# Two attention layers on one core: eighth score ahead of the fourth mixing, input piece issued a half earlier

## The chip, the cores and the metric

The program runs on one core of a Trainium2 chip, in one launch. The metric is the device time of that launch in microseconds, the median of several executions. The engines named are TensorE (PE, its weight loads PEld), VectorE (DVE), ScalarE (ACT), GpSimd (POOL) and SyncE (SP), which issues nearly all DMA transfers.

## The reference, cut to what matters

Eight images of 512 channels and 32 x 32 positions (T = 1024) pass through two attention layers with 8 heads of 64 channels. Each layer is given a group normalization of its input, and its result is added to the input. All is float32. The first layer is ordinary softmax attention with its own second normalization. The second one, in which the change lies, mixes the heads' scores before the softmax and normalizes the softmax's result over each image and head:

```
q, k, v = w_q @ y, w_k @ y, w_v @ y                     # y: normalized input, split in 8 heads
attn = einsum('bhdq,bhdT->bhqT', q, k) * scale          # scores
attn = einsum('gh,bhqT->bgqT', w_head, attn)            # mixing of the heads
attn = softmax(attn, axis=-1)
attn = (attn - mean(attn)) / sqrt(var(attn) + eps) * in_gamma + in_beta   # per image and head
out  = einsum('bhqT,bhdT->bhqd', attn, v)
x    = x + w_proj @ out + b_proj
```

## The kernel before, in words

**Layer 2's loop.** An outer loop runs over the eight images (instances). For each, an object `Attention1` works in blocks `p` of 128 queries, eight blocks and a last round that only finishes. A block is cut into four quarters `t`; the method `step(p, t, ag)` (line 1847) writes out by hand what is issued in a quarter. The order in that text is the order in which each engine gets its instructions; there is no planner. Three blocks are in flight at once: `step(p, ...)` makes the scores of block `p`, mixes and exponentiates block `p - 1`, and multiplies blocks `p - 1` and `p - 2` by the values. An `Agenda` calls further work (projections of values, normalizations of the next image, projection of its keys) at numbered slots between the quarters.

**Scores.** `scores(p, i)` (line 1621) makes the eighth part `i` of a block's scores: for two heads, against one half `kh` of the 1024 keys. Parts 0 to 3 are the first half, 4 to 7 the second. Each takes a two-bank tile of PSUM from a ring of three tiles (`m_psum`, pool `ps1_m`), and ScalarE copies it into the tile `raw[kh]` in SBUF (line 1640).

**Regrouping.** In the mixing the heads have to lie on partitions. So `regroup(p, kh, s)` (line 1642) issues two DMA transfers of 256 KB from `raw[kh]` into a slot of the tile `re_t`; four values of `s` make up a half. A half can only go out when the copies of its four scores are done, since each transfer reads from all of them. The first half's slots go round five places, the second half's are four fixed ones, so a transfer of the second half waits until the mixing of the block before has read that slot. At the end of quarter 1 the first half's first three slots are issued, at the end of quarter 2 the fourth, at the end of quarter 3 the second half's four. All go through the SP queue, in order.

**Mixing.** `mix(p, s)` (line 1656) multiplies the regrouped scores with the mixing weights. It takes two tiles of the same ring of three, and ScalarE makes the exponentials of each (line 1678) into a tile `e` of a ring of two. VectorE transposes them (`flip`, line 1686) and takes their moments (`moments`, line 1698). In the kernel before, `mix` issues the matmuls and the first tile's exponential, and returns a function that issues the second tile's exponential, so that the caller can put something between the two. The mixing `mix(p - 1, 0)` is issued in quarter 0, after three scores of block `p` and 64 products of the values; it needs slot 0 of both halves, the second of which was issued at the end of the quarter before.

**Pieces.** `piece()` (line 1650) issues one transfer from a list: for each image but the last, the four parts of the next image's input (`y_piece`, line 1333) and two parts of the weights for its keys (`left_piece`, line 1302), 512 KB each; for the last image four parts of the projection's weights (`p_piece`, 256 KB each). One is issued in each block from `p = 1` until the list is empty. The input's tile has one buffer, and the parts are normalized from slot 20 on, that is from quarter 0 of block 5.

The other transfers of a block are a small one and its broadcast of 256 KB on POOL's queue (lines 1772 and 1779).

Of the kernel before, what the change touches and what calls it, by code (L numbers as in the profile page):

```python
# [467 lines left out]
def tile_two_attention_layers(  # L468
# [798 lines left out]
    with ExitStack() as l1:  # L1267
# [15 lines left out]
        def m_psum(nm):  # L1283
            return ps_m.tile([P, 2, FB], F32, tag="m", name=nm)
# [156 lines left out]
        def k_leave():  # L1441
            for fn in due:
                fn()
            due.clear()
# [168 lines left out]
        class Attention1:  # L1613
# [42 lines left out]
            def mix(self, p, s):  # L1656

                b = self.b
                first = (4 * p + s) % NF
                halves = re_t[:, first : NF + s + 1 : NF + s - first]  # L1660
                ps = [m_psum(f"m1_{b}_{p}_{s}_{h}") for h in range(2)]
                for c in range(4):
                    for a in range(4):
                        rows = slice(a * 32, a * 32 + 32)
                        nc.tensor.matmul(  # L1665
                            ps[a // 2][c * 32 : c * 32 + 32, a % 2].rearrange(
                                "p (r h k) -> p h r k", r=2, h=2
                            ),
                            wmix[rows].rearrange("p g i -> p (g i)"),
                            halves[rows].rearrange(  # L1670
                                "p h r (kb c k) -> p c h (r kb) k", c=4, k=32
                            )[:, c],
                            start=True, stop=True, tile_position=(a * 32, c * 32),
                        )
                e = self.e[p, s] = epool.tile([P, 2, 4, 2 * P], F32, tag="e", name=f"e1_{b}_{p}_{s}")

                def exponentials(h):
                    nc.scalar.activation(  # L1678
                        e[:, :, 2 * h : 2 * h + 2].rearrange("p r a k -> p a r k"),
                        ps[h].rearrange("p a (r k) -> p a r k", r=2), AF.Exp,  # L1680
                    )

                exponentials(0)
                return lambda: exponentials(1)

            def flip(self, p, s):

# [159 lines left out]
            def step(self, p, t, ag):  # L1847

                new, old, older = p < NT, p >= 1, p >= 2
                if t == 0:  # L1850
                    if new:
                        for i in range(3):
                            self.scores(p, i)
                    if older:
                        self.values(p - 2, 0, 2, 3)
                        self.leave(p - 2, 0)
                        self.sums(p - 2)
                        if p % 2 == 0 and p >= 4:
                            self.divide(p // 2 - 2, nc.gpsimd)
                    if old:  # L1860
                        self.mix(p - 1, 0)()
                    ag.run(4 * p - 0.5)
                elif t == 1:
                    if older:
                        self.values(p - 2, 1, 0)
                        self.flip(p - 1, 0)
                        self.totals(p - 2)
                        self.moments(p - 1, 0)
                    if new:
                        self.scores(p, 3)  # L1870
                    if old:
                        self.mix(p - 1, 1)()
                    ag.run(4 * p + 0.5)
                elif t == 2:
                    if older:
                        self.values(p - 2, 1, 1)
                    if new:
                        self.scores(p, 4)
                        self.scores(p, 5)
                    if old and not new:  # L1880
                        self.mix(p - 1, 2)()
                    ag.run(4 * p + 1.5)
                    if older:
                        self.values(p - 2, 1, 2, 3)
                        self.leave(p - 2, 1)
                    if old and new:
                        self.mix(p - 1, 2)()
                else:
                    if new:
                        self.scores(p, 6)  # L1890
                        if old:
                            self.values(p - 1, 0, 0)
                            second = self.mix(p - 1, 3)
                        self.scores(p, 7)
                        if old:
                            second()
                            self.values(p - 1, 0, 1)
                    else:
                        self.mix(p - 1, 3)()
                        self.values(p - 1, 0, 0, 1)  # L1900
                    ag.run(4 * p + 2.5)
                k_leave()
                if p == 1 or old and t:
                    self.flip(p - 1, t)
                    self.moments(p - 1, t)
                if new:
                    for kh, s in (
                        (), ((0, 0), (0, 1), (0, 2)), ((0, 3),), ((1, 0), (1, 1), (1, 2), (1, 3)),
                    )[t]:
                        self.regroup(p, kh, s)  # L1910
                if old and t == 2:
                    self.piece()
                ag.run(4 * p + t)

# [155 lines left out]
```

## Time and profile before

| what | value |
|---|---|
| median of 3 runs | 4051.5 us (4041.93 to 4057.18) |
| the profiled execution | 4047.25 us |
| its span, first to last instruction | 4045.5 us |
| granted TensorE clock | 0.994 |
| busy: TensorE, VectorE, ScalarE, GpSimd | 3895.9, 2833.2, 1966.6, 128.5 us |
| layer 2 (from its first regrouping) | from 1806 us on |
| HBM read and written | 197.16 and 46.92 MB |

Rows in the profile give a start in us from the span's beginning, a duration, the engine, the line in the kernel, the operation, what it writes and reads, and how many instructions are merged (x8). A bracket at the end is the idle time of that engine before the row, with what ended it. "SPq" rows are DMA issues. A row of a group on the page has the busy time, the mean duration in ns of one instruction, and after the bar the idle time before such instructions. Matmul rows count the passes that a float32 product takes, so one score of 4 products has 8. Shares are averages over layers with different limits: VectorE's 70% is 21.00 us of the 22.25 us from 2753.75 to 2776.00, a block of layer 2, in which the DMA engines' mean share is 0.93.

### The profile page before, as it was taken

How to read it: one execution, taken by the hardware profiler on the slowest of the kernel's cores; microseconds unless marked ns; L12 is line 12 of the kernel's file. 1: busy time of each engine (PE TensorE's matmuls, PEld its weight loads, DVE VectorE, ACT ScalarE, POOL GpSimd, SP SyncE). 2: the span in 40 equal slices, each digit the busy share in tenths (PEclk: the TensorE clock that was granted, in tenths of full speed). 3: DMA queues.
4: the chain of work that ended last, by engine and by line, in shares of the span. 5: the costliest groups of instructions: out<-in, count | busy, mean ns of one | idle time of the engine just before them, and what ended most of it. 6: DMA issues, size and time to landing. Idle time of an engine off the chain costs nothing. (4 is left out here: it accounts for less than half of the span.)

```text
span 4045.5 us, 95879 instructions
## 1 busy us (share of the span) xinstructions
PE 3895.9 (96%) x41932; PEld 1835.3 (45%) x41932; DVE 2833.2 (70%) x4124; ACT 1966.6 (49%) x2431; POOL 128.5 (3%) x150
## 2 busy tenths in 40 slices
PE   8999999999999999999999999999999999999997
PEld 4353535343444435334544545545544445445354
DVE  4748475756666575747848858759769679588597
ACT  1717263545445362616517537437257166175274
POOL 0000000000000000000000000000001000000010
PEclk9999999999999999999999999999999999999998
DMA  3313131211111211228638638559468287386384
GB/s 126 112 47 116 45 118 48 87 51 54 66 66 58 77 54 61 77 84 208 184 115 213 197 109 221 169 136 226 144 169 221 96 210 202 109 218 189 109 219 125
DMA packets 245884, 519.10 MB, mean 128 GB/s; under 512 B 47313, under 2 KB 54481, under 8 KB 238801
## 3 DMA queue, kind: packets, MB, share of 16 engines
q1 hardware_dynamic: 238912, 497.95, 42.9%
q0 software_dynamic: 6544, 14.94, 1.7%
q8 instruction: 331, 5.42, 0.6%
q14 instruction: 97, 0.79, 0.1%
HBM read 197.16 MB, written 46.92 MB: 60 GB/s over the span
## 5 line engine op out<-in xcount | busy, mean ns | idle before, releaser
L1693 DVE STREAM_TRANSPOSE et<-e 128x2048 f32<-128x2048 f32 x256 | 587.4, 2294 | 137.1 <-ACT e L1678 131.8
L1720 PEld LDWEIGHTS a<-et,v 128*64 128x64 f32 x16384 | 512.0, 139 | 296.7 <-issue 230.8
L1704 DVE BATCH_NORM_STATS2 bn<-e 128x6 f32<-128x512 f32 x1024 | 633.9, 675 | 0.0
L1089 ACT ACTIVATE e<-s 128x1024 f32<-128x1024 f32 x512 | 497.2, 1026 | 234.0 <-PE s L1084 231.9
L1678 ACT ACTIVATE e<-m 128x1024 f32<-128x1024 f32 x512 | 502.9, 1023 | 203.0 <-issue 94.6
L1720 PE MATMUL a<-et,v 128*64 128x64 f32 x16384 | 560.4, 225 | 14.8 <-DVE et L1693 10.4
L1640 ACT COPY raw<-s 128x1024 f32<-128x1024 f32 x480 | 470.1, 1018 | 205.8 <-PE s L1628 172.6
L1097 DVE TENSOR_TENSOR zacc<-zacc,e 128x1024 f32<-128x1024 f32 x384 | 468.8, 1221 | 90.4 <-ACT e L1089 68.1
L1628 PE MATMUL s<-k,q 64*64 64x512 f32 x4096 | 515.8, 608 | 6.3 <-DVE q L1493 3.1
L1084 PE MATMUL s<-q,k 64*64 64x512 f32 x4096 | 490.1, 593 | 2.3 <-ACT e L1089 2.3
L1110 PE MATMUL a<-e,v 64*64 64x512 f32 x4096 | 484.1, 589 | 0.0
L1665 PE MATMUL m<-re,wmix 32*32 32x512 f32 x8192 | 322.7, 605 | 81.4 <-DMA re<-raw 67.8
L1110 PEld LDWEIGHTS a<-e,v 64*64 64x64 f32 x4096 | 156.7, 133 | 282.8 <-issue 282.2
L1084 PEld LDWEIGHTS s<-q,k 64*64 64x64 f32 x4096 | 147.9, 133 | 275.1 <-issue 240.5
L1628 PEld LDWEIGHTS s<-k,q 64*64 64x64 f32 x4096 | 128.1, 132 | 263.7 <-issue 98.7
L1454 PE MATMUL pv<-wv,y 128*128 128x512 f32 x480 | 212.1, 597 | 0.0
L1736 ACT COPY q<-a 64x256 f32<-64x256 f32 x256 | 93.8, 366 | 179.2 <-PE a L1720 177.0
L1665 PEld LDWEIGHTS m<-re,wmix 32*32 32x32 f32 x8192 | 73.5, 103 | 171.6 <-ACT e L1678 53.3
L1772 POOL DMA_DIRECT2D zd<-rz x56 | 34.7, 619 | 3476.0 <-DVE r L1784 3476.0
L1454 PEld LDWEIGHTS pv<-wv,y 128*128 128x128 f32 x480 | 89.3, 190 | 116.9 <-issue 110.3
L1458 ACT COPY v<-pv 128x512 f32<-128x512 f32 x30 | 17.6, 585 | 218.7 <-PE pv L1454 218.7
L1095 DVE TENSOR_TENSOR zacc<-e,e 128x1024 f32<-128x1024 f32 x64 | 78.3, 1223 | 57.2 <-ACT e L1089 57.2
(315 smaller groups left out, 3944.6 us busy)
## 6 DMA issues: line engine op xcount, KB each, us to landing
re<-raw SPq DMA_DIRECT2D x1024, 256.0 KB
left_q<-left_q SPq DMA_DIRECT2D x17, 1792.0 KB
left_p<-left_p SPq DMA_DIRECT2D x17, 1792.0 KB
left_k<-left_k SPq DMA_DIRECT2D x10, 1792.0 KB
x<-in_x_dram SPq DMA_DIRECT2D x32, 512.0 KB
rzb<-zd SPq DMA_DIRECT2D x128, 128.0 KB
x<-x SPq DMA_DIRECT2D x64, 256.0 KB
y<-x SPq DMA_DIRECT2D x32, 512.0 KB
```

The source lines that it names most:

```text
L1084: nc.tensor.matmul(ps[c * D : c * D + D, m], k[r, hp, k0 : k0 + D], q[r, hp, ts(f, FB)], start=True, stop=True,)
L1089: nc.scalar.activation(e[i], ps, AF.Exp, scale=S0 * S0)
L1097: nc.vector.tensor_add(zacc[g], zacc[g], e[i])
L1110: nc.tensor.matmul(acc[g][a][m * D : m * D + D], v[rows, kc, ts(2 * hp + m, D)], e[i][rows, m], start=(kc == 0), stop=(kc == NG - 1),)
L1454: nc.tensor.matmul(ps[:, m], y_t[b][:, c, ts(2 * i + m, P)], w[:, c], start=(c == 0), stop=(c == NCC - 1),)
L1628: nc.tensor.matmul(ps[c * D : c * D + D, m], qo_t[b][r, p, hp, ts(c, D)], k_t[b][r, hp, ts(kh, FB)], start=True, stop=True,)
L1640: nc.scalar.copy(dst, ps)
L1665: nc.tensor.matmul(ps[a // 2][c * 32 : c * 32 + 32, a % 2].rearrange("p (r h k) -> p h r k", r=2, h=2), wmix[rows].rearrange("p g i -> p ( ...
L1678: nc.scalar.activation(e[:, :, 2 * h : 2 * h + 2].rearrange("p r a k -> p a r k"), ps[h].rearrange("p a (r k) -> p a r k", r=2), AF.Exp,)
L1693: nc.vector.transpose(self.et[p, u].rearrange("p kb (r st a) g q -> p st kb r (a g q)", r=2, st=2)[:, st], self.e[p, s].rearrange("p r a ( ...
L1704: nc.vector.bn_stats(self.bn[p][:, s, a], e[:, :, a].rearrange("p r k -> p k r"))
L1720: nc.tensor.matmul(acc[two * D : two * D + D, s].rearrange("p (x q) -> p x q", q=4), v_t[b][:, kb, ts(g, D)], et[:, kb, :, g], start=(kb = ...
```

## The change

Two things move; nothing is added or taken away.

- In quarter 3, the order of issue becomes: score 6, values, score 7, fourth mixing, values. Before it was score 6, values, fourth mixing, score 7, values, with the second exponential of that mixing held back until after score 7. The function that `mix` returned is gone, and both exponentials are issued by `mix` itself everywhere; in the other quarters this is the same order as before. On ScalarE the last quarter's order becomes copy 6, copy 7, exponential, exponential, instead of copy 6, exponential, copy 7, exponential.
- The piece is issued in quarter 0 instead of quarter 2. On the SP queue, it stood between a block's first-half regrouping (8 transfers) and its second-half regrouping (8 transfers). Now it stands ahead of the block's first half, right behind the second half of the block before.

On VectorE and GpSimd the order of the instructions is unchanged.

```diff
                 exponentials(0)
-                return lambda: exponentials(1)
+                exponentials(1)
...
                     if old:
-                        self.mix(p - 1, 0)()
+                        self.mix(p - 1, 0)
...
                 else:
                     if new:
                         self.scores(p, 6)
                         if old:
                             self.values(p - 1, 0, 0)
-                            second = self.mix(p - 1, 3)
                         self.scores(p, 7)
                         if old:
-                            second()
+                            self.mix(p - 1, 3)
                             self.values(p - 1, 0, 1)
                     else:
-                        self.mix(p - 1, 3)()
+                        self.mix(p - 1, 3)
                         self.values(p - 1, 0, 0, 1)
...
-                if old and t == 2:
+                if old and t == 0:
                     self.piece()
```

More of the change, by code (lines that the diff above doesn't have):

```diff
@@ L1871, in step @@
                     if old:
-                        self.mix(p - 1, 1)()
+                        self.mix(p - 1, 1)
                     ag.run(4 * p + 0.5)
@@ L1880, in step @@
                     if old and not new:
-                        self.mix(p - 1, 2)()
+                        self.mix(p - 1, 2)
                     ag.run(4 * p + 1.5)
@@ L1886, in step @@
                     if old and new:
-                        self.mix(p - 1, 2)()
+                        self.mix(p - 1, 2)
                 else:
```

## The prediction

> **What bounds the kernel now.** I read the page first (engine shares, then the costliest groups), then the waits, then the timelines of layer 1, where all of the change lies. Page:
>
> ```profile
> PE 3895.9 (96%) x41932; PEld 1835.3 (45%) x41932; DVE 2833.2 (70%) x4124; ACT 1966.6 (49%) x2431; POOL 128.5 (3%) x150
> ...
> L1665 PE MATMUL m<-re,wmix 32*32 32x512 f32 x8192 | 322.7, 605 | 81.4 <-DMA re<-raw 67.8
> ```
>
> TensorE hardly rests, and the one large idle item in its rows is the mixing's, released by the regrouping DMA. TensorE's timeline of one block (instance 3; the block's last quarter begins at 2768.31 with the seventh score, the next block's first quarter at 2773.75):
>
> ```profile
> 2768.31 1.11 PE L1628 MATMUL s<-k,q 64*64 64x512 f32 x8
> 2769.35 1.15 PE L1720 MATMUL a<-et,v 128*64 128x64 f32 x32
> 2770.43 1.29 PE L1665 MATMUL m<-re,wmix 32*32 32x512 f32 x32
> 2771.64 1.09 PE L1628 MATMUL s<-k,q 64*64 64x512 f32 x8
> 2772.66 1.15 PE L1720 MATMUL a<-et,v 128*64 128x64 f32 x32
> 2773.75 2.81 PE L1628 MATMUL s<-k,q 64*64 64x512 f32 x24
> 2776.48 2.08 PE L1720 MATMUL a<-et,v 128*64 128x64 f32 x64
> 2780.07 1.15 PE L1665 MATMUL m<-re,wmix 32*32 32x512 f32 x32 [1.50 <-DMA re<-raw]
> ```
>
> Everything runs back to back except before the block's first mixing at 2780.07. ScalarE and the SP queue show why:
>
> ```profile
> 2768.58 1.94 ACT L1678 ACTIVATE e<-m 128x1024 f32<-128x1024 f32 x2 [0.48 <-ACT q L1736]
> 2770.41 1.02 ACT L1640 COPY raw<-s 128x1024 f32<-128x1024 f32 x1
> 2771.89 1.02 ACT L1678 ACTIVATE e<-m 128x1024 f32<-128x1024 f32 x1 [0.46 <-PE m L1665]
> 2772.80 1.01 ACT L1640 COPY raw<-s 128x1024 f32<-128x1024 f32 x1
> ```
> ```profile
> 2765.93 5.04 SPq L1646 DMA_DIRECT2D re<-raw  x4
> 2771.02 1.26 SPq L1337 DMA_DIRECT2D y<-x  x1
> 2773.84 18.20 SPq L1646 DMA_DIRECT2D re<-raw  x16
> ```
>
> The eighth score's copy ends at 2773.81 and the second half's regrouping is issued at 2773.84; the 512 KB input piece went in 2.82 us before it. The mixing starts 6.23 us after that issue. I call its idle time the boundary wait, measured as the start-to-start gap less the usual 0.15. Over the 56 boundaries that follow a changed quarter, the timelines give 61.1 us for the first six of each instance (48 waits; median 1.41, longest 2.77) and 23.0 us for the seventh (2.9 each; it has no next scores as cover): 84 us, 2% of the span.
>
> **What the Trainium skill says.** "Perfetto Trace Analysis", section Tensor Engine Instruction: ScalarE and VectorE are strict FIFO. The trace agrees: the eighth copy (2772.80) stands behind an exponential (2771.89), although its score began at 2771.64. "DMA: Bandwidth & Descriptors", section Queues, rings and completion order: each DMA engine takes a ring's descriptors in order, and engines finish a DMA independently. The trace agrees: with a 512 KB piece ahead, issue to mixing took 5.2 to 7.4 us, mostly about 6; at the seventh boundaries, without one, mostly 4.4 to 4.7, and 5.2 to 5.4 in two of eight. "PSUM — Partial Sum Buffer", section Specifications: eight 2 KiB banks; three two-bank score/mixing tiles and two one-bank tiles fill them, so the ring of three stays. No run here shows that count.
>
> **Part 1: eighth score ahead of the fourth mixing.** No instruction is added. On TensorE the order becomes score 7, values, score 8, mixing 4, values. A gap depends on what it follows (0.15 after values, 0.52 after a score or a mixing, start to start), so the sum of the quarter is the same. Score 8 moves to 2770.43; its last product starts 0.50 later and a copy follows a score's last start by 0.65 (2782.44 + 0.50 to 2783.59), so copy 8 is ready at 2771.58. ScalarE is free of copy 7 at 2771.43. Copy 8 then ends at 2772.60 and the regrouping goes out at 2772.63: **1.2 us earlier** (rounded from 1.21).
>
> What is pushed back: mixing 4 starts at 2771.45. The ring of three gives score 8 the first tile of mixing 3 (exponential done by 2769.6), and mixing 4 the second tile of mixing 3 (done by 2770.52) and score 7's (copied by 2771.43). Its second tile is wanted at 2771.50 and released about 0.11 after the copy's end, 2771.54: 0.04 us of stall, against the 0.15 that mixing 4 loses now to the exponential before it (0.70 instead of 0.55 to issue). Free, with 0.1 us of cover; a longer delay costs its length 56 times, since values, the next three scores and the boundary mixing are queued behind it on TensorE. Exponentials 4 run 2772.75 to 2774.80, where they end at 2774.74 now; VectorE's transpose of them starts at 2775.53 after other work. Behind them on ScalarE are the next block's copies, 2775.93. The last regrouping of the half waits for mixing 4 to have read its slot (about 2772.7), but is not issued before about 2776.5.
>
> **Part 2: the piece.** On SP it moves from between the two halves to ahead of the first half, so right behind the previous block's second half. 46 pieces (six of 512 KB in each of seven instances, four of 256 KB in the last) leave the queue in front of the 8 regroupings. In the solid stretch after 2776, about 2 MB moved in 7 us, 0.29 MB a us: 1.8 us a piece. Its new cover: DMA share falls to 0.07 in 2784.0 to 2785.5. Second half 2.1 MB (7.2 us) from 2773.8, piece 1.8, ends by about 2783; the next first half is issued at 2784.6 now and about 2783.1 with the wait gone. If that cover is gone, the first half has until the next boundary, over 10 us. SP's own issue (0.8 us) falls before a wait for a copy. Each transfer also waits on SP for the eighth one before it; for the piece that is the half's first, landed by then. The first piece overwrites a buffer that a value projection (7 us of TensorE, right behind the half's last score) reads last; SP issues the half for some 5 us of that, and behind the piece only the next first half queues, which has no data yet.
>
> **Sum.** Mixing can begin at 2778.57, 5.9 us after the new issue; without a piece ahead it needs about 4.5. So the first six waits go: 61.1. Left over: nine waits above 1.9 us, cut by 1.8 to 1.9 where only the piece sets the landing, 2; one wait of 1.65 in the last instance with no piece ahead, 1. VectorE takes some: between a block's first transposes its work is 20.1, 20.2, 20.8, 21.2, 20.3 us in blocks 1 to 5, TensorE without waits about 20.7 to 21.4. It idles on the exponential of the same mixing:
>
> ```profile
> 2783.38 2.31 DVE L1693 STREAM_TRANSPOSE et<-e 128x2048 f32<-128x2048 f32 x1 [1.71 <-ACT e L1678]
> ```
>
> Where its idle time is the smaller of the two, mostly blocks 3 and 4 with a normalization, the difference is lost: 3. At the seventh boundary VectorE does not idle in the first seven instances (subtractions for the next projection follow), so 2.9 down to 1.7 on TensorE buys nothing there; in the last it idles 1.7, so 1.2 gained. 61.1 - 2 - 1 - 3 + 1.2 = **56 us**. I take off 2 for TensorE's own 1.3 us "issue" pauses, a few of which the waits now absorb (both ends: 0 to 8): 54. The profiled execution took 4047.25 us (span 4045.5): 3993. The median of the runs is 4.25 above: 4051.5 - 54 = **3997.5**.
>
> **Rivals.**
> 1. Half the gain. VectorE's 70% hides that it is within 1 us of TensorE in layer 1; if its lag spreads, or the earlier half runs into the first half's tail (in the shown block the queue never emptied), half the 1.2 us shift without the piece's help gives 26: 4025. Against: the shift in full without the piece gives 46.6 (each wait cut by up to 1.22), and the piece alone nearly 59.
> 2. No effect, 4045 to 4055: the waits reappear whole as another engine's. Against: VectorE's idle time before its first transpose (10.9 us per instance over six blocks) exceeds the waits (7.6).
> 3. Slower: mixing 4 waits for copy 7, which stands behind mixing 3's exponentials. If copy 7 ended 1.0 us later than here, 56 x 1.0 eats the gain; at 1.5 us (a 1.24 us normalization in front of it on ScalarE, say) the kernel takes 4051.5 + 56 x 1.5 - 54 = 4081. Against: copy 7's end relative to the issue is -2.41 in nearly every block, and its earliest cause, the exponentials, runs back to back.
> That copy 8 does not get earlier is excluded unless ScalarE is late in the same way.
>
> **How the numbers follow.** Main case 0.72, 3985 to 4013 (gain 54, -14 to +12 for the pauses, the lag and the runs' spread of 4042 to 4057). Rival 1 0.14, rival 2 0.07, rival 3 0.07. A measurement of this kernel tells 0.5% (20 us) from no change. Faster: 0.72 + 0.12 = 0.84; same 0.09; slower 0.07. For 8 in 10 the main case's range is stretched upward into rival 1: 3983 to 4027.
>
> **What would show it.** Right: second-half regrouping issued right after two copies in a row, 1.2 us sooner; boundary gaps at 0.15 for most first-six boundaries, about 1.7 at the seventh; idle time behind the regrouping DMA down from 67.8 to under 20; VectorE's wait for the exponential shrinking with it; block periods near 21. Wrong: gaps before mixing 4 beyond 0.15, a new wait of ScalarE or VectorE of the same size, or issue-to-mixing staying at 6 us.

## The result and the profile after

The changed kernel takes 4000.18 us, the median of four runs (3994.73 to 4001.58). The kernel before, run beside it, takes 4052.86 (4041.93 to 4057.18). The ratio is 0.9872 with a 95% interval of 0.985 to 0.9893: 52.7 us less. The profiled execution of the changed kernel has a span of 3997.5 us, against 4045.5 before, so the two traces hold 48.0 us of the difference.

The page of the changed kernel (busy time and share of each engine, then groups: busy us, mean ns of one, and after the bar the idle time before them):

```profile
PE 3885.5 (97%) x41932; PEld 1826.1 (46%) x41932; DVE 2834.6 (71%) x4124; ACT 1971.3 (49%) x2431; POOL 128.5 (3%) x150
...
L1693 DVE STREAM_TRANSPOSE et<-e 128x2048 f32<-128x2048 f32 x256 | 587.3, 2294 | 88.7 <-ACT e L1678 86.8
...
L1665 PE MATMUL m<-re,wmix 32*32 32x512 f32 x8192 | 315.3, 604 | 19.3 <-DMA re<-raw 17.8
```

The mixing's idle time behind the regrouping DMA fell from 67.8 to 17.8 us. VectorE's wait for the exponentials fell too, and that figure of before has not been shown yet. The page of the kernel before:

```profile
L1693 DVE STREAM_TRANSPOSE et<-e 128x2048 f32<-128x2048 f32 x256 | 587.4, 2294 | 137.1 <-ACT e L1678 131.8
```

Here is the last quarter of a block in the changed kernel and the block's boundary. It is the same instance as the one shown of before. First TensorE's timeline:

```profile
2757.76 1.11 PE L1628 MATMUL s<-k,q 64*64 64x512 f32 x8
2758.80 1.15 PE L1720 MATMUL a<-et,v 128*64 128x64 f32 x32
2759.88 1.09 PE L1628 MATMUL s<-k,q 64*64 64x512 f32 x8
2760.90 1.17 PE L1665 MATMUL m<-re,wmix 32*32 32x512 f32 x32
2762.01 1.15 PE L1720 MATMUL a<-et,v 128*64 128x64 f32 x32
2763.09 2.81 PE L1628 MATMUL s<-k,q 64*64 64x512 f32 x24
2765.82 2.08 PE L1720 MATMUL a<-et,v 128*64 128x64 f32 x64
2767.84 1.14 PE L1665 MATMUL m<-re,wmix 32*32 32x512 f32 x32
2769.04 1.15 PE L1720 MATMUL a<-et,v 128*64 128x64 f32 x32
2772.27 0.39 PE L1757 MATMUL z<-sel,zz 128*64 128x32 f32 x4 [2.08 <-DVE zz L1750]
2772.59 1.82 PE L1628 MATMUL s<-k,q 64*64 64x512 f32 x8
```

Then ScalarE and the SP queue at the same place:

```profile
2759.86 1.02 ACT L1640 COPY raw<-s 128x1024 f32<-128x1024 f32 x1
2761.04 1.01 ACT L1640 COPY raw<-s 128x1024 f32<-128x1024 f32 x1 [0.16 <-PE s L1628]
2762.25 1.94 ACT L1678 ACTIVATE e<-m 128x1024 f32<-128x1024 f32 x2 [0.19 <-PE m L1665]
```
```profile
2762.08 6.97 SPq L1646 DMA_DIRECT2D re<-raw  x8
2769.09 1.22 SPq L1306 DMA_DIRECT2D left_k<-left_k  x1
```

The two copies stand together. The second half goes out at 2762.08, 4.32 us after the seventh score began (before: 2773.84 less 2768.31, 5.53). The mixing at 2767.84 follows the values without a pause. The piece comes behind the half. Its new place has no price that shows: all of the 17.8 us that mixings still wait for the regrouping are at the boundaries.

The pause that catches the eye is the one at 2772.27. The small product for the softmax's totals (line 1757, tile `z`) waits 2.08 us for the sums that VectorE makes (line 1750, tile `zz`). In the waits of TensorE this is now the largest. The changed kernel (us in total, times, longest):

```profile
PE z L1757 <- DVE zz L1750: 29.1, 27, 2.1
PE m L1665 <- DMA re<-raw: 17.8, 11, 3.3
```

The kernel before:

```profile
PE z L1757 <- DVE zz L1750: 4.9, 9, 0.8
```

VectorE's timeline shows why the sums were late:

```profile
2765.26 1.50 DVE L692 TENSOR_SCALAR y<-y,gmean,grstd 128x1024 f32<-128x1024 f32 x1
2766.68 2.30 DVE L1693 STREAM_TRANSPOSE et<-e 128x2048 f32<-128x2048 f32 x1
2768.91 2.47 DVE L1704 BATCH_NORM_STATS2 bn<-e 128x6 f32<-128x512 f32 x4
2771.41 0.22 DVE L1746 TENSOR_SCALAR zz<-bn 128x64 f32<-128x64 f32 x1
```

It works without a gap. A normalization for the next image stands in front, and TensorE, no longer held up at the boundary, arrives at the totals before it.

Counted as the prediction counts (start-to-start gaps less the usual ones), the two traces differ as follows. The boundary waits are those of the 56 boundaries, the fourth mixings are all 64, and the totals are those of blocks 0 to 5, which have scores behind them:

| TensorE's lost time, us | before | after | difference |
|---|---|---|---|
| boundary waits, first six per instance | 61.1 | 1.7 | -59.4 |
| boundary waits, seventh | 23.0 | 17.2 | -5.8 |
| fourth mixing, beyond its 0.55 us of issue | 7.6 | 2.6 | -5.0 |
| rows of values that last longer than usual ("issue" pauses and others) | 8.5 | 1.5 | -7.0 |
| totals waiting for VectorE's sums | 9.1 | 38.8 | +29.7 |
| sum of these rows | 109.3 | 61.8 | -47.5 |

Of 65 us of waits removed at the boundaries, 30 came back at another place. (With the last instance's block 6, which the row leaves out, it is 32: its totals wait 2.0 us in the changed kernel and 0.05 before.)

### The profile page after: what moved, and what is told of

Read it like the earlier page. It is cut to its first block, busy times and chain, and to the rows that moved or that the text cites. A ratio compares the mean times of both kernels' runs of the same rounds, so it can differ in the third digit from the quotient of the medians.

```text
span 3997.5 us, 95841 instructions
## 1 busy us (share of the span) xinstructions
PE 3885.5 (97%) x41932; PEld 1826.1 (46%) x41932; DVE 2834.6 (71%) x4124; ACT 1971.3 (49%) x2431; POOL 128.5 (3%) x150
## 4 chain that ended last, share of the span: by engine, by line
PE 81%; DVE 13%; ACT 2%; DMA 2%; issue 2%; SPq 0%; DVEq 0%
PE s L1084 11%; PE a L1110 11%; PE a L1720 7%; PE s L1628 7%; DVE bn L1704 6%; PE pk_p L902 6%; PE pq_p L902 5%; PE pv L1454 5%; PE pv_p L902 5%; DVE et L1693 5%; PE pp_p L902 5%; PE pk L1379 4%; PE pq L1379 4%; PE pp L1379 4%; PE m L1665 4%
## 5 line engine op out<-in xcount | busy, mean ns | idle before, releaser
L1693 DVE STREAM_TRANSPOSE et<-e 128x2048 f32<-128x2048 f32 x256 | 587.3, 2294 | 88.7 <-ACT e L1678 86.8
L1720 PE MATMUL a<-et,v 128*64 128x64 f32 x16384 | 557.0, 225 | 12.1 <-DVE et L1693 11.4
L1665 PE MATMUL m<-re,wmix 32*32 32x512 f32 x8192 | 315.3, 604 | 19.3 <-DMA re<-raw 17.8
```

What stands on the lines that cost most here:

```text
L1665: nc.tensor.matmul(ps[a // 2][c * 32 : c * 32 + 32, a % 2].rearrange("p (r h k) -> p h r k", r=2, h=2), wmix[rows].rearrange("p g i -> p ( ...
L1693: nc.vector.transpose(self.et[p, u].rearrange("p kb (r st a) g q -> p st kb r (a g q)", r=2, st=2)[:, st], self.e[p, s].rearrange("p r a ( ...
L1720: nc.tensor.matmul(acc[two * D : two * D + D, s].rearrange("p (x q) -> p x q", q=4), v_t[b][:, kb, ts(g, D)], et[:, kb, :, g], start=(kb = ...
```

## The experiments

All were timed against the kernel before, in several comparisons, so that kernels of different comparisons are compared by their ratios. The table has what the sections below use. "Issue" is the time from the seventh score's start to the issue of the second half's regrouping, "to mixing" the time from there to the boundary mixing. Over the 48 first-six boundaries, issue is the median (at an instance's first boundary it is some 0.6 us longer in every kernel) and to mixing the mean. The waits are counted as above, each in one trace. That of the piece alone is its fastest run (4007.04 us), 10 us below its median, so its waits may be low.

| kernel | median us | ratio, 95% interval | issue | to mixing | first six | seventh | fourth mixing | totals |
|---|---|---|---|---|---|---|---|---|
| before | 4052.86 | 1 | 5.53 | 5.92 | 61.1 | 23.0 | 7.6 | 9.1 |
| after | 4000.18 | 0.9872 (0.985 to 0.9893) | 4.31 | 5.79 | 1.7 | 17.2 | 2.6 | 38.8 |
| score alone | 4050.35 | 0.9982 (0.9974 to 0.9989) | 4.31 | 7.17 | 67.9 | 21.7 | 2.9 | 6.7 |
| piece alone | 4017.46 | 0.9906 (0.9891 to 0.9922) | 5.53 | 4.79 | 7.0 | 22.3 | 8.1 | 30.3 |
| ScalarE's order alone | 4049.45 | 0.9987 (0.9978 to 0.9995) | 5.53 | 5.87 | 45.9 | 23.5 | 9.3 | 12.3 |
| after, piece ahead of the second half | 4051.14 | 0.999 (0.9982 to 0.9998) | 4.31 | 7.08 | 62.3 | 19.8 | 3.5 | 8.2 |
| after, once more | 4003.34 | 0.988 (0.9863 to 0.9898) | 4.31 | 5.78 | 2.2 | 19.5 | 2.6 | 37.7 |
| after, totals later | 3970.12 | 0.9799 (0.9783 to 0.9815) | 4.31 | 5.81 | 2.3 | 19.1 | 4.0 | 0.1 |
| before, totals later | 4032.32 | 0.9947 (0.993 to 0.9964) | 5.53 | 5.68 | 49.5 | 25.1 | 9.6 | 0.1 |
| piece alone, totals later | 3999.49 | 0.9855 (0.9838 to 0.9872) | 5.53 | 5.00 | 16.1 | 23.9 | 10.6 | 0.1 |

A time to mixing can't fall below what TensorE has to do until it arrives: 4.7 us with the old order, 5.75 with the new one. Where it stands at that value, the half had landed earlier, and the number says only "by then".

**The score alone.** The changed kernel with the piece back in quarter 2:

```diff
-                if old and t == 0:
+                if old and t == 2:
                     self.piece()
```

> Only the eighth score and the fourth mixing change places; the piece stays between the two halves. My theory (the boundary wait is issue time plus what stands ahead in the DMA rings, and either half of the change removes most of it): the second half goes out 1.2 us earlier, each of the first six boundary waits is cut by up to 1.22 us, 61.1 falls to about 15, and part of it is given back on VectorE's sums, so 4010 to 4020 us, about 0.991 of before. Rival (the piece alone does it, because the rings' backlog and not the issue sets the landing): issue to mixing grows to over 7 us, the waits stay, within 10 us of before.

Measured: 0.9982, that is 7 us. The half goes out 1.22 us earlier (5.53 to 4.31), and the time to the mixing grows by 1.25 (5.92 to 7.17). On the mean the landing does not move. The page of this run:

```profile
L1665 PE MATMUL m<-re,wmix 32*32 32x512 f32 x8192 | 321.9, 608 | 87.2 <-DMA re<-raw 78.9
```

Here the earlier issue was worth next to nothing while the queue in front was full. The DMA engines' mean share is 0.97 in the 6 us ahead of the mixing at 2780.07 in the kernel before (2773.8 to 2780.0). That fits a half that lands when the bytes ahead of it, and its own, have been moved, whenever it was put in.

**The piece alone.** The kernel before with the piece in quarter 0:

```diff
-                if old and t == 2:
+                if old and t == 0:
                     self.piece()
```

> Only the piece moves; the order of the last quarter is that of before. My theory: the second half goes out at the old time, but issue to mixing falls from about 6 to 4.7 us, which is just what TensorE has as cover; the first six waits fall from 61.1 to under 10, the seventh stay at 2.9, and mixing 4 keeps its 0.15 us; 4005 to 4018 us, about 0.990. Rival (the shift of 1.2 us does it): within 10 us of before.

Measured: 0.9906, 38 us, most of the gain. The boundary waits go from 61.1 to 7.0, and the totals' wait appears here already (9.1 to 30.3). Page of this run:

```profile
L1665 PE MATMUL m<-re,wmix 32*32 32x512 f32 x8192 | 321.4, 605 | 28.9 <-DMA re<-raw 25.4
```

So the two parts do not add up: 7 us and 38 us apart, 52 together. Once the piece is gone from in front, the score's move takes another 5.3 (first six), 5.1 (seventh) and 5.5 us (fourth mixing) from TensorE's waits; against that the totals wait 8.5 us longer. That leaves 7.4 us, as between these two traces (spans 4005.3 and 3997.5); by the ratios it is about 14.

**ScalarE's order alone.** The kernel before, with both exponentials of the fourth mixing issued after the eighth copy. TensorE's and SP's orders are those of before.

```diff
-                exponentials(0)
-                return lambda: exponentials(1)
+                def both():
+                    exponentials(0)
+                    exponentials(1)
+                return both
```

> TensorE's and SP's orders are those of before; on ScalarE alone both exponentials of the fourth mixing follow the eighth copy. If the eighth copy was late because it stood behind an exponential, as the prediction reads the timeline, it starts about 0.9 us earlier and some 30 us are gained. If it was late because its score was (last product at 2772.14, plus 0.65 is 2772.79, the very time at which the copy began), the copy starts where it did, and the time is within 0.3% of before, or a little worse, since the first exponential comes a us later.

Measured: 0.9987, some 5 us. The half's issue stays at 5.53: the eighth copy does not come earlier when the exponential ahead of it is gone. It was its own score that it waited for. The boundary waits shrink by 15, but not because data come sooner: TensorE arrives 0.24 us later at each boundary (10.43 instead of 10.19 us after the seventh score). That is 11.5 us over 48 boundaries, paid elsewhere. The eighth score starts when it did, 3.33 us after the seventh. The next block's first three scores are the ones that slip, the first from 5.43 to 5.56 us and the third from 7.20 to 7.40. Their tiles are those of the fourth mixing and the eighth score, and the first of them is now released a copy later.

**The piece in front of the second half.** The changed kernel with the piece issued at the end of quarter 3, right ahead of the second half:

```diff
+                if old and t == 3:
+                    self.piece()
                 if new:
                     for kh, s in (
...
-                if old and t == 0:
-                    self.piece()
```

> The changed kernel, but the piece is issued at the end of the last quarter, right ahead of the second half's regrouping. My theory (each ring is served in order, 512 KB cost 1.8 us, and SP's issue 0.8 us): the mixing can start about 0.8 + 1.8 + 4.5 = 7.1 us after the eighth copy, against 5.8 without a wait, so 46 waits of about 1.3 us come back, 45 to 60 us, less what VectorE's wait gives up: 4030 to 4055 us. Rival (the transfers' order does not matter at this load): within 8 us of the changed kernel, 3992 to 4008.

Measured: 0.999. Nearly the whole gain is gone, with the copies and the issue still early (4.31). SP queue and TensorE of this run:

```profile
2788.31 1.29 SPq L1306 DMA_DIRECT2D left_k<-left_k  x1
2791.09 7.02 SPq L1646 DMA_DIRECT2D re<-raw  x8
```
```profile
2799.44 1.15 PE L1665 MATMUL m<-re,wmix 32*32 32x512 f32 x31 [2.52 <-DMA re<-raw]
```

This run tests less than was meant. After the first half's last regrouping SyncE has nothing to issue until the second half, and the piece does not wait for the eighth copy. So it goes out as soon as the queue comes to it, 2.8 us before the half (2788.31 and 2791.09), as with the score alone (2798.14 and 2800.96 at the same boundary). In the two traces every engine has the same instructions in the same order, and SyncE the same transfers. The run is a repetition of the score alone and agrees with it: 4051.14 and 4050.35 us, to mixing 7.08 and 7.17. The first-six waits are 62.3 and 67.9, so such a sum can differ by 5 us or so between executions of one order. The expected 7.1 us was met by luck: it has 0.8 for SP's issue of the piece, which lies before the wait for the copy. A piece that leaves only when the eighth copy is done was not run.

What remains is one order, run twice, beside the changed kernel, from which it differs in the piece's place alone. From the seventh score the mixing comes 11.4 us later in all three kernels that have the piece in front (before 11.45, score alone 11.48, this one 11.39), and after 10.10 without it. "DMA: Bandwidth & Descriptors" in the Trainium skill (Queues, rings and completion order) says that an engine takes a ring's descriptors in order. The three sums agree with it: behind the piece, the half lands at one time, whether it was issued 5.53 or 4.31 us after the seventh score.

**The totals later.** Score 4 and the second mixing stand behind the totals' product on TensorE, and need nothing from it. "TensorE: Matmul & The Clock Gate" (The mechanism) says that matmuls start and complete in program order. The pause at 2772.27 agrees: score 4 begins only at 2772.59, 0.32 us after the totals. So I moved the totals and the moments issued with them behind these two. VectorE's order of instructions stays the same.

```diff
                     if older:
                         self.values(p - 2, 1, 0)
                         self.flip(p - 1, 0)
-                        self.totals(p - 2)
-                        self.moments(p - 1, 0)
                     if new:
                         self.scores(p, 3)
                     if old:
                         self.mix(p - 1, 1)
+                    if older:
+                        self.totals(p - 2)
+                        self.moments(p - 1, 0)
```

The changed kernel once more, to stand beside it on the same chip:

> The changed kernel itself, so that the next two runs have it beside them on the same chip. Every theory: 0.985 to 0.990 of the kernel before, 3994 to 4004 us, boundary waits of the first six under 4 us, TensorE's totals waiting 30 to 45 us for VectorE's sums.

Measured: 0.988, with 37.7 us at the totals; the first result repeats. Then the move on top of the change:

> The changed kernel with TensorE's small product for the totals moved behind score 4 and mixing 2 of the same quarter, some 2.4 us of TensorE work; VectorE's order is the same. Theory (the new wait at the totals is lost time of TensorE, since score 4 and mixing 2 need nothing from VectorE): the wait of 39 us falls under 8, and the kernel gains 20 to 38 us on the changed one, 3962 to 3982. Rival (VectorE is the bound in the blocks where TensorE waits for its sums; whatever TensorE does first, it waits later for VectorE's transposes, and VectorE in turn now waits up to 2 us for the totals that it divides by): the wait moves, the kernel stays within 8 us of the changed one, 3990 to 4010, and the idle time of the values' products behind VectorE's transposes rises by about 30 us.

Measured: 3970.12 us, 0.9799 of the kernel before, 33 us faster than the changed kernel in the same comparison. The totals' wait is gone and did not come back. A wait of TensorE in this run, its timeline around the totals, and VectorE's idle time from the page:

```profile
PE a L1720 <- DVE et L1693: 13.7, 16, 5.3
```
```profile
2742.07 1.09 PE L1628 MATMUL s<-k,q 64*64 64x512 f32 x8
2743.09 1.30 PE L1665 MATMUL m<-re,wmix 32*32 32x512 f32 x32
2744.33 0.36 PE L1757 MATMUL z<-sel,zz 128*64 128x32 f32 x3
```
```profile
L1693 DVE STREAM_TRANSPOSE et<-e 128x2048 f32<-128x2048 f32 x256 | 586.4, 2291 | 57.0 <-ACT e L1678 56.5
```

The values' products wait 13.7 us for VectorE's transposes instead of 11.4, where the rival wanted 30 more. VectorE's wait for exponentials falls again, from 86.8 to 56.5. So VectorE was not the bound of the blocks as a whole. It idled for exponentials that TensorE could not deliver, because TensorE stood waiting for VectorE's sums: each waited for the other in turn, and independent work stood behind. Block 4, in which VectorE has the most to do, is the exception. From its first transpose to the next block's, VectorE idles 0.2 us in both kernels, and the time stays (21.5 us, and 21.6 with the totals later). The gain lies mainly in blocks 1 and 5, where VectorE idled 2.0 and 2.4 us and now 0.9 and 0.4 (22.0 to 20.8 us, 22.6 to 20.4). On VectorE a transpose of 2.3 us lies between the sums and the first use of the totals (line 1769), so the product has that long before anyone misses it.

The same move in the kernel before:

> The same move in the kernel before, where the totals wait only 9 us. Theory: at most 9 us gained, 4043 to 4053, since its blocks are held up by the boundary waits and VectorE has slack. If it gains 20 us or more, the late totals are worth something that has nothing to do with the change. Rival (VectorE's wait for the totals costs by itself): 5 to 20 us slower, 4057 to 4072.

Measured: 4032.32 us, 0.9947, 21 us faster and thus more than the 9 us of wait that it removes. The trace has 9.0 us of it at the totals, 5 or so in the long rows of values, which is within chance (see the second profile below), and 11.6 in the first-six boundary waits, while the other rows grow by 4. Why the boundary waits shrink there (to mixing 5.68 instead of 5.92) I did not find out. By my own bound the late totals are worth something apart from the change, so not all of the 33 us need be owed to the wait that the change made.

And with the piece alone:

> The kernel before with two moves only: the piece issued in quarter 0, and the totals' product behind mixing 2; the eighth score stays behind the fourth mixing. It asks whether the score's move is still worth anything once the totals no longer stand in front. Theory (it takes waits of its own off TensorE: boundary waits 7.0 to 1.7 us, seventh 22.3 to 17.2, the fourth mixing's 8.1 to 2.6): about 16 us slower than the kernel with all three moves (3970), 3982 to 3992. Rival (the totals' wait was the place where VectorE's lag came out, and without it the score's move has nothing to save): within 6 us of 3970.

Measured: 0.9855. The kernel with all three moves has 0.9799, so the score's move is worth 0.56%, about 23 us: more than the 14 us that the same move is worth with the totals in front (0.9906 to 0.9872), and more than the 16 that I had worked out. In the table the difference lies in the boundary waits (16.1 and 23.9 against 2.3 and 19.1) and the fourth mixing (10.6 against 4.0), together 25 us. I read it so, without a run that tests it: with the old order a shorter block leaves the half too little time (first six 7.0 to 16.1, when the totals no longer hold TensorE back), and the new order has 1.2 us in hand.

**A second profile of the kernel before**, to know what single profiles can tell:

> The kernel before once more, for a second profile of it: how much do its boundary waits (61.1 us) and its pauses of TensorE (8.5 us) differ from execution to execution? Theory: under 8 us in the waits, so that the 45.9 and 49.5 us of two experiments with the old place of the piece are effects of their edits. Rival: they differ by 10 us or more of themselves, and differences of that size between single profiles say nothing.

Measured: 62.1 us of boundary waits instead of 61.1, 8.5 at the totals instead of 9.1, 7.6 at the fourth mixing both times; but 3.6 us of long rows of values instead of 8.5. Here the waits repeat (the two runs of the score alone's order differ by more, 5.6 us). The pauses are chance, and of the 7.0 us in the first table some 5 must be left out of any reasoning.

## Why the prediction was right, and where it was not

The time and its main cause came out as forecast. Its steps follow. ("Layer 1" in the prediction is the second layer, counted from 0.)

**The 1.2 us shift** (part 1): 1.21 forecast, 1.22 measured, 5.53 to 4.31.

**The fourth mixing**: right in size and not used. The text gives 0.04 us of stall instead of 0.15. The trace has 2.6 us over 64 mixings, 0.04 each, instead of 7.6. The difference, some 0.1 us times 56, was called free and left out of the sum: 5.0 us.

**The piece's 1.8 us** (part 2): with it in front the mixing starts 11.4 us after the seventh score, without it at 10.1 or earlier, where TensorE only then arrives. That bounds the price at 1.3 us or more. The 1.8 is also mis-worked: from 2776 to 2783 the trace of before has 255 GB/s, so 1.79 MB and not 2, and 512 KB take 2.1 us at that rate. Both figures agree with the bound, and no run measures the price. Issue to mixing with a 512 KB piece ahead is 4.70 to 7.43 us in the timelines, below the 5.2 to 7.4 of the text in four of 42.

**The first-six waits**: 61.1 less 3 left over, so 58.1 forecast; 59.4 measured.

**"At the seventh boundary [...] buys nothing"**: not what the trace shows. The seventh waits fell from 23.0 to 17.2 us, or 19.5 in the repetition, 2.1 to 2.4 each where 1.7 was forecast. TensorE's own gain there was to come to nothing except in the last instance, 1.2; how much of it reached the end no run tells apart.

**VectorE "takes some [...] 3"**: the term that failed. The totals wait 29.7 us longer, ten times that. The reasoning missed the mechanism, too. It compared VectorE's work per block with TensorE's and charged the shortfall of idle time. That holds for block 4 alone. On the whole, the kernel with later totals shows that VectorE could keep up: the same work in blocks of 20.8 us on the mean of blocks 1 to 4, where the changed kernel has 21.3. Most of the loss sat in the order of TensorE's queue, in a product that needs fresh sums and stands in front of others that don't. The prediction's timeline breaks off at the boundary mixing (2780.07). This product comes next but one, at 2782.14, where an earlier TensorE had to run into it, and I did not cost it.

**The pauses, 2 us lost**: none lost that shows; the term is inside what two profiles of one kernel differ by.

**The sum**: 54 us forecast, 52.7 measured. That it came out so near is luck, because errors cancelled: about 27 us too little charged for VectorE, against the fourth mixing (5.0), the seventh boundaries (up to 4.6) and the pauses uncredited, with the two executions' own differences on top (the span's gain is 48.0).

**Rival 1** did not occur, but the argument against it rests on a false step: "the shift in full without the piece gives 46.6 (each wait cut by up to 1.22)". The shift without the piece gave 7 us. Behind the piece the earlier issue did not move the landing, and the prediction's own sentence about a ring's order could have told that. "The piece alone nearly 59" holds for the waits (54.1 gone), not for the time (38), for the same totals.

**The reading of ScalarE's order**: the eighth copy does stand behind an exponential, but that did not delay it. Its score's last product starts at 2771.64 + 0.50 = 2772.14, and 0.65 later is 2772.79; the copy starts at 2772.80. ScalarE's order alone left the issue at 5.53. The sum did not lean on that reading.

**Rival 2** (the waits reappear whole) had the right mechanism at half its size: 30 of 65 us. **Rival 3** did not occur: the fourth mixing waits less than before.

**What would show it**: second half behind two copies, 1.2 us sooner, yes; idle time behind the DMA under 20, yes (17.8); first-six gaps at the usual value, 44 of 48. One sign of being wrong could not tell: "issue-to-mixing staying at 6 us". It did stay (5.92 to 5.79), because TensorE itself now arrives only 5.75 us after the earlier issue. Block periods near 21 hold for blocks 2 to 4 (21.0 to 21.3). Block 5 stands out with 23.1, longer than the 22.7 of before, and was the sign of the totals' wait, the largest of all blocks there (14.4 of the 38.8 us).

## What to carry to other kernels

When a wait for a DMA has been found, ask first whether the queue ahead of the transfer is full: if it is, as here, take bytes from in front of it first, and see only then what an earlier issue pays. When a wait is taken from an in-order engine, walk down that engine's queue and ask of each next instruction whether its input will be there that much earlier; the first one that is not ready is the new wait, whatever the busy shares say. If independent work stands behind it, swapping the two can be worth as much as the change itself (here 33 us against 52).

## What the runs showed of the hardware that was not expected

**Half clock after short waits.** After the 2.08 us pause of TensorE in the changed kernel, its next score took 1.82 us instead of 1.09. The granted clock in stretches of 1 us there (the columns after the time: length, busy time of TensorE, its weight loads, VectorE, ScalarE and GpSimd, granted clock, DMA share, GB/s):

```profile
2772.00:2773.00 1.00, 0.73 (x8) 0.52 (x12) 1.00 (x2) 0.00 (x0) 0.00 (x0) 0.90 0.94 330
2773.00:2774.00 1.00, 1.00 (x8) 0.00 (x0) 1.00 (x1) 0.00 (x0) 0.00 (x0) 0.50 0.26 94
2774.00:2775.00 1.00, 1.00 (x20) 0.28 (x32) 0.96 (x5) 0.54 (x1) 0.13 (x1) 0.50 0.02 8
2775.00:2776.00 1.00, 1.00 (x32) 0.00 (x0) 0.97 (x3) 0.47 (x1) 0.51 (x1) 0.50 0.07 16
2776.00:2777.00 1.00, 1.00 (x40) 0.72 (x26) 1.00 (x3) 0.45 (x1) 0.00 (x0) 0.89 0.40 70
```

Half rate for about 3.4 us costs 1.7 us on top of the pause, if half of that time is taken as lost. "TensorE: Matmul & The Clock Gate" (What's actually happening) puts the drop after an idle window of about 3.4 us. Here it also followed shorter pauses, one of 2.1 us and one of 1.4 (at 2812.6, with 0.4 a little before), though another of 2.1 us in the same trace brought none. From 1850 to 3985 us the kernel before has nine such stretches, each at a boundary wait of 2.0 to 3.5 us. Of its ten pauses above 2.2 us eight brought one, of 21 between 1.4 and 2.2 us only one. So the length of a pause does not decide alone, but it weighs. The second profile of before has seven stretches, the two profiles of the changed kernel five each. A few last 6.8 us; together they last 30.7 us in both profiles of before, and 23.9 and 20.5 in those of the changed kernel. The prediction had no term for it; half of the difference is 3.4 to 5.1 us. Part of that is in the table above already: three of its long rows of values, 0.73 us each at 1946.7, 2188.5 and 3653.0, are values at half clock and no pauses.
